# Output projection by seven products of quarters; quarter sums and a mask on GpSimd, layer 0's statistics on ScalarE

## The chip, the cores and the metric

The kernel runs on one core of one Trainium2 chip. The metric is the device time of one execution in microseconds. Each core has a matmul engine (TensorE, PE in the profile, with its weight loads listed as PEld), VectorE (DVE), ScalarE (ACT), GpSimd (POOL) and the queue of SyncE (SP), which issues transfers. Each works through its own instructions in order, and they wait for one another by semaphores.

## The reference

```python
def reference(x, adj, W, a_src, a_dst, Wq, bq, Wk, bk, Wv, bv, Wo, bo):   # x: (64, 256, 512) f32
    # layer 0: graph attention over 256 nodes, one head
    h = relu(layernorm(x))
    Wh = h @ W
    logits = leaky_relu((Wh @ a_src)[:, :, None] + (Wh @ a_dst)[:, None, :], 0.2)
    x = x + softmax(where(adj == 0, -inf, logits)) @ Wh
    # layer 1: 8 heads of 64, masked by adj
    h = relu(layernorm(x))
    q, k, v = heads(h @ Wq.T + bq), heads(h @ Wk.T + bk), heads(h @ Wv.T + bv)
    attn = softmax(where(adj == 0, -inf, q @ k.T / 8))
    return x + concat(attn @ v) @ Wo.T + bo
```

All arithmetic is in f32. The layer norm has no weights (eps 1e-5).

## The kernel before

One batch element g (256 tokens, two tiles of 128, four chunks of 128 features) is the unit of work; there are G = 64. Each stage is a Python generator (`normalize0`, `weights0`, `aggregate0`, `transform0`, `normalize1`, `transpose1`, `project_qk`, `project_v`, `attention`, `scale`, `output`) that issues the instructions of one step and yields. The lists `period`, `second`, `first` and `last` write out by hand in what order the steps of five batches in flight are issued; TensorE, VectorE, ScalarE and the SP queue keep that program order (`tc.manual_schedule(engines=...)`). A period is one pass through the lists. The letters: K is one of seven steps of `project_qk` for batch i, V one of seven of `project_v`, W one of four halves of layer 0's transform for i+1, O a step of `output` for i-2, N0, E0, U0 layer 0's statistics and normalization, edge weights and aggregation for i+2, N1, X1 layer 1's normalization and transposes for i+1, A and A_OLD the attention of i and of i-1.

q, k and v are made by a scheme of seven products (`products`): the left matrix and the weight are each cut into 2 x 2 quarters, `combine_w` makes sums of the weight's quarters once, `combine` makes four sums of the left's quarters per batch (128x256 each, all in SBUF), and `add_up` puts the seven results together on VectorE, which reads them from PSUM. Of `project_qk`'s products, number 0 and number 4 are read by ScalarE first, with a bias. For number 4, ScalarE writes the tile p5 (line 576), and VectorE then makes two additions from it (lines 203 and 204). The output projection is not done so before: `output` computes it with plain products, four halves (steps O) per batch, and adds each 128x512 result to the residual x (line 704), then stores it.

`normalize0` uses VectorE's batch-norm statistics (lines 99, 100), a power on GpSimd (line 106), ScalarE's normalizing ReLU (line 418) and four multiply-and-sum instructions on VectorE (line 425), which give the node scores es and ed. `weights0` begins with two TensorE transposes of es (line 439, the tile pe), then takes exponents on ScalarE, the maximum, the mask (line 453) and the sum of two halves (line 455) on VectorE. `attention` multiplies the exponents with the mask (line 627) and sums two halves (line 629) on VectorE; line 687 (`scale`) applies the reciprocals to aT. GpSimd also adds the output bias to x (line 551), in `transpose1`.

All PSUM tiles come from one pool of eight banks. The parts of the schedule that matter here:

```python
second = [
    W, N1, E0, K, W, W, N1, A_OLD, A, N1, E0, A, V, A, V, V, V, V, U0, V, V,
    X1, U0, X1, U0, X1, U0, A, A, (scale, -1),
]
period = [(load, 3), A_OLD, K, A_OLD, O, K, O, N0, K, O, N0, K, O, N0, K, W, K] + second
```

Of the kernel before, what the change touches and what calls it, by code (L numbers as in the profile page):

```python
# [9 lines left out]
F32 = mybir.dt.float32  # L10
# [6 lines left out]
P = 128  # L17
# [11 lines left out]
def kernel(  # L29
# [71 lines left out]

    def inverse_std(mv, nm, small):
        ve = small.tile([P, NT], F32, tag="ve", name=f"ve{nm}")
        nc.vector.tensor_scalar_add(ve, mv[:, :, 1], EPS)  # L104
        rstd = small.tile([P, NT], F32, tag="rstd", name=f"rstd{nm}")
        nc.gpsimd.tensor_tensor(rstd, ve, minus_half, op=ALU.pow)  # L106
        return rstd

    def norm_stats(xt, nm, small):

        mv = small.tile([P, NT, 2], F32, tag="mv", name=f"mv{nm}")
        for t in range(NT):
            token_stats(mv[:, t, :], xt[:, t, :], f"{nm}_{t}", small)
        return mv, inverse_std(mv, nm, small)

# [16 lines left out]
    def bounded():  # L132
# [10 lines left out]

        def load_w(src, name):
            t = weights.tile([P, DC, D], F32, tag=name, name=name)
            nc.sync.dma_start(t, src.rearrange("(c p) e -> p c e", p=P))
            return t

        def load_quarters(src, name):
# [17 lines left out]
        def combine(a, name):  # L167

            s = work.tile([P, 4, DC // 2, P], F32, tag=name[0], name="_".join(name))
            nc.vector.tensor_add(s[:, 0], a(1, 0), a(1, 1))  # L170
            nc.vector.tensor_sub(s[:, 1], s[:, 0], a(0, 0))  # L171
            nc.vector.tensor_sub(s[:, 2], a(0, 0), a(1, 0))
            nc.vector.tensor_sub(s[:, 3], a(0, 1), s[:, 1])
            return s
# [60 lines left out]
        load_group(0)  # L235
        w_sb = load_w(w, "w_sb")
        a_rows = [work.tile([P, D], F32, tag=f"aT{j}", name=f"a_row_{j}", bufs=2 - j) for j in range(2)]
# [7 lines left out]
        load_group(2)  # L245
        wo_sb = load_w(woT, "wo_sb")
        wv_sb = load_quarters(wvT, "wv_sb")
# [42 lines left out]
        def prepare_qk():  # L290
# [4 lines left out]
            combine_w(wk_sb)  # L295

        def output_bias():

            pb = bank([P, D], "pbias")
            for c in range(DC):  # L300
                nc.tensor.matmul(
                    pb,
                    cols["bv"][:, c : c + 1].to_broadcast([P, P]),
                    wo_sb[:, c, :],
                    start=(c == 0),
                    stop=(c == DC - 1),
                )
            nc.vector.tensor_add(bo_b, pb, bo_b)

        def constants():  # L310


            def whole(wt, src, nm):
                b12 = work.tile([P, DC // 2, HD], F32, tag="b12", name=f"b12_{nm}", bufs=2)
                nc.gpsimd.dma_start(b12, quarter_of(src, 0, 1))
                return ((wt[:, B11], b12), (wt[:, B21], wt[:, B22]))

# [79 lines left out]
            nc.vector.tensor_reduce(okm, ok, AX.X, ALU.min)  # L397
            yield
            pk = bank([1, 1], "pok")
# [5 lines left out]
        def normalize0(g):  # L405

            xt = xts[g]
            mv, rstd = norm_stats(xt, f"0_{g}", small)
            nmr = small.tile([P, NT], F32, tag="nmr", name=f"nmr_{g}")
            yield  # L410
            nc.vector.scalar_tensor_tensor(  # L411
                nmr, mv[:, :, 0], -1.0, rstd, op0=ALU.mult, op1=ALU.mult
            )
            h = big.tile([P, NT, D], F32, tag="h", name=f"h_{g}", bufs=2)
            es = small.tile([P, NT], F32, tag="es", name=f"es_{g}")
            ed = small.tile([P, NT], F32, tag="ed", name=f"ed_{g}")
            for t in range(NT):
                nc.scalar.activation(  # L418
                    h[:, t, :], xt[:, t, :], AF.Relu, bias=nmr[:, t : t + 1], scale=rstd[:, t : t + 1]
                )  # L420
            yield
            for t in range(NT):
                for dst, a in ((es, 0), (ed, 1)):
                    junk = work.tile([P, D], F32, tag="junk", name=f"junk_{g}_{t}")
                    nc.vector.scalar_tensor_tensor(
                        junk, h[:, t, :], 1.0, wa[a], op0=ALU.mult, op1=ALU.mult,
                        accum_out=dst[:, t : t + 1],
                    )
            edl = small.tile([P, NT], F32, tag="edl", name=f"edl_{g}")
            nc.vector.tensor_scalar_mul(edl, ed, NEG_SLOPE)  # L430
            nodes[g] = h, es, ed, edl
            yield

        def weights0(g):
# [17 lines left out]
            em = work.tile([P, NC, N], F32, tag="em", name=f"em_{g}", bufs=2)  # L452
            nc.vector.tensor_mul(em, e1, maskT)  # L453
            esum = work.tile([P, N], F32, tag="esum", name=f"esum_{g}")
            nc.vector.tensor_add(esum, em[:, 0, :], em[:, 1, :])
            edges[g] = em, esum
            yield

        def aggregate0(g):
# [26 lines left out]
            nc.vector.reciprocal(rs, rs)  # L486

            sums0[g] = uT, rs
            yield

        def project_half(dst, left, w_t, t, n):
# [23 lines left out]
        def normalize1(g):  # L515
            xt = xts[g]
            mv = small.tile([P, NT, 2], F32, tag="mv", name=f"mv1_{g}")
            for t in range(NT):
                token_stats(mv[:, t, :], xt[:, t, :], f"1_{g}_{t}", small)
                if t == 0:  # L520
                    yield
            rstd = inverse_std(mv, f"1_{g}", small)
            yield
# [12 lines left out]
        def transpose1(g):  # L536
            xn = norms.pop(g)
            hT = big.tile([P, DC, TOK], F32, tag="hT", name=f"hT_{g}")

            def a(t, j):  # L540
                return hT[:, 2 * j : 2 * j + 2, t * P : (t + 1) * P]

            for t in range(NT):
                pt = bank([P, DC, P], f"pt_{g}_{t}")
                for c in range(DC):
                    nc.tensor.transpose(pt[:, c, :], xn[:, t, c * P : (c + 1) * P], ident)
                nc.scalar.activation(hT[:, :, t * P : (t + 1) * P], pt, AF.Relu)
                yield
            lefts[g] = a, combine(a, ("hs", str(g)))
            for t in range(NT):  # L550
                nc.gpsimd.tensor_tensor(xts[g][:, t, :], xts[g][:, t, :], bo_b, op=ALU.add)  # L551
            yield
# [48 lines left out]
        def attention(g):  # L601
# [47 lines left out]
            for j in range(2):  # L649
                pair = [scores(2 * j + i) for i in range(2)]  # L650
                yield
                for i in range(2):
                    sums.append(masks(2 * j + i, pair[i]))
                    yield
                values(j, pair)
                if j == 0:
                    yield
# [26 lines left out]
        def scale(g):  # L684
# [3 lines left out]

            outs[g] = aT
            yield  # L690

        def output(g):
            xt = xts.pop(g)
            aT = outs.pop(g)

            def left(c, t):
                return aT[c // 2][:, c % 2, t * P : (t + 1) * P]

            for t in range(NT):
                po = bank([P, D], f"po1_{g}_{t}")  # L700
                project_half(po, left, wo_sb, t, 0)
                yield
                project_half(po, left, wo_sb, t, 1)
                nc.vector.tensor_add(xt[:, t, :], po, xt[:, t, :])  # L704
                row = (g * NT + t) * P
                nc.sync.dma_start(out_rows[row : row + P, :], xt[:, t, :])
                yield

# [20 lines left out]
        def aside(n=1):  # L729
# [8 lines left out]
        second = [  # L738
            W, N1, E0, K, W, W, N1, A_OLD, A, N1, E0, A, V, A, V, V, V, V, U0, V, V,
            X1, U0, X1, U0, X1, U0, A, A, (scale, -1),  # L740
        ]
        period = [(load, 3), A_OLD, K, A_OLD, O, K, O, N0, K, O, N0, K, O, N0, K, W, K] + second
        last = [A_OLD, A_OLD, A_OLD, O, O, O, O, (scale, -1)]


        steps((normalize0, 0), (normalize0, 0))
        node_weights()
        edge_mask()
        steps((normalize0, 0), (weights0, 0))
        aside()  # L750
        steps((normalize0, 1), (weights0, 0), (aggregate0, 0), (aggregate0, 0))
        prepare_qk()
        steps((aggregate0, 0), (aggregate0, 0), (normalize0, 1), (transform0, 0), (transform0, 0))
        steps((normalize1, 0), (transform0, 0), (transform0, 0), (normalize1, 0))
        aside(2)
# [4 lines left out]
        first = [  # L760
            (load, 3), K, (normalize0, 1), K, (weights0, 1), K, N0, K, (weights0, 1), N0, K,
            (aggregate0, 1), (aggregate0, 1), N0, K, (aggregate0, 1), (aggregate0, 1), W,
        ]
        for i in range(G + 2):
            for n, (stage, ahead) in enumerate(last if i == G else period if i else first + second):
# [217 lines left out]
```

## Time and profile before

| | us |
|---|---|
| median of three runs | 3026.2 (3024.74 to 3027.28) |
| the profiled execution's own time | 3028.91 |
| its span, from first to last instruction | 3027.1 |
| PE busy | 2987.1 (99%) |
| PEld busy | 2184.2 (72%) |
| DVE busy | 2124.1 (70%) |
| ACT busy | 941.3 (31%) |
| POOL busy | 296.5 (10%) |

The granted TensorE clock is 0.998 of full speed over the span. Rows of groups read: line, engine, operation, tiles written and read, shapes, count, then busy time and mean duration of one in ns, then the idle time before them. Rows of the timeline read: start and length in us from the span's start, engine, line, operation, tiles, shape, how many instructions are merged in the row, and in brackets the idle time before them with what ended it. One period of the steady state is 46.18 us: GpSimd's additions of line 551 start at 964.36 us and again at 1010.54 us.

### The profile page before, as it was taken

The page shows a single profiled execution, that of the slowest core. Times are in us where ns is not written, and L with a number is a line of the kernel's source. Part 1 is how long each engine was busy: PE and PEld are TensorE (multiplying, and loading weights), DVE is VectorE, ACT ScalarE, POOL GpSimd, SP SyncE. Part 2 cuts the span into 40 slices and gives each one's busy share as a digit, 9 for nine tenths or more (in the row PEclk, how much of TensorE's full clock was granted, in tenths as well). Part 3 has the DMA queues.
Part 4 walks back from the last instruction along what each step waited for, and adds up shares of the span by engine and source line. Part 5 has one row for each costly group of instructions (what it writes and reads, how often), then busy time and mean ns, then how long its engine had stood idle before and what let it go on. Part 6 is the DMA issues. An engine that isn't in the chain of part 4 may idle for free. (4 is left out here: it accounts for less than half of the span.)

```text
span 3027.1 us, 45790 instructions
## 1 busy us (share of the span) xinstructions
PE 2987.1 (99%) x18166; PEld 2184.2 (72%) x18166; DVE 2124.1 (70%) x4110; ACT 941.3 (31%) x2011; POOL 296.5 (10%) x279
## 2 busy tenths in 40 slices
PE   7999999999999999999999999999999999999998
PEld 5777777777777777777777777777777777777775
DVE  6767767767777677677677677776776776777764
ACT  2333323323333333233233333332332333333321
POOL 1100101101101101011011011010110110110100
PEclk9999999999999999999999999999999999999999
DMA  3112212212212122122122122221221221222213
GB/s 125 18 30 41 36 28 39 39 29 39 31 36 36 31 40 36 29 39 39 28 39 33 35 36 32 39 36 29 42 36 29 39 38 30 38 32 38 29 23 42
DMA packets 82062, 110.79 MB, mean 37 GB/s; under 512 B 11762, under 2 KB 47602, under 8 KB 81842
## 3 DMA queue, kind: packets, MB, share of 16 engines
q1 hardware_dynamic: 81122, 105.95, 21.9%
q8 instruction: 145, 2.38, 0.3%
q0 software_dynamic: 720, 1.85, 0.2%
q14 instruction: 75, 0.61, 0.1%
HBM read 40.64 MB, written 33.55 MB: 25 GB/s over the span
## 5 line engine op out<-in xcount | busy, mean ns | idle before, releaser
L493 PE MATMUL po<-wo_sb,aT 128*128 128x512 f32 x1024 | 483.0, 595 | 4.7 <-DVE aT L687 4.7
L493 PE MATMUL po<-w_sb,uT 128*128 128x512 f32 x1024 | 470.9, 593 | 0.0
L627 DVE TENSOR_TENSOR ex<-ex,maskT 128x512 f32<-128x512 f32 x512 | 397.0, 816 | 7.1 <-ACT ex L622 1.4
L221 PEld LDWEIGHTS pqk<-hs,wq_sb 128*128 128x128 f32 x2048 | 263.5, 192 | 90.3 <-issue 89.4
L106 POOL TENSOR_TENSOR rstd<-ve,minus_half 128x2 f32<-128x2 f32 x128 | 89.5, 699 | 2379.4 <-DVE ve L104 2379.4
L622 ACT ACTIVATE ex<-psc 128x512 f32<-128x512 f32 x512 | 264.4, 602 | 126.3 <-PE psc L614 126.3
L493 PEld LDWEIGHTS po<-w_sb,uT 128*128 128x128 f32 x1024 | 180.1, 191 | 154.4 <-issue 154.4
L493 PEld LDWEIGHTS po<-wo_sb,aT 128*128 128x128 f32 x1024 | 176.0, 192 | 132.6 <-issue 129.8
L221 PE MATMUL pqk<-hs,wq_sb 128*128 128x128 f32 x2048 | 270.1, 275 | 0.7 <-DVE hs L171 0.7
L221 PE MATMUL pqk<-hs,wk_sb 128*128 128x128 f32 x2048 | 270.5, 275 | 0.0
L510 DVE SCALAR_TENSOR_TENSOR x<-po,rs,x 128x512 f32<-128x512 f32 x128 | 96.1, 751 | 238.5 <-PE po L493 238.5
L614 PE MATMUL psc<-qk 64*128 64x256 f32 x2048 | 255.7, 389 | 0.0
L212 PE MATMUL pv<-wv_sb,hs 128*128 128x256 f32 x1024 | 254.5, 381 | 0.0
L221 PEld LDWEIGHTS pqk<-hT,wq_sb 128*128 128x128 f32 x1536 | 196.2, 191 | 80.4 <-issue 59.3
L639 PE MATMUL pav<-ex,v 128*64 128x256 f32 x2048 | 250.9, 386 | 3.0 <-DVE ex L627 2.4
L221 PEld LDWEIGHTS pqk<-hs,wk_sb 128*128 128x128 f32 x2048 | 249.3, 192 | 0.0
L468 PE MATMUL pu<-em,h 128*128 128x256 f32 x1024 | 241.9, 379 | 1.7 <-DVE em L453 1.0
L418 ACT ACTIVATE h<-x,nmr,rstd 128x512 f32<-128x512 f32 x128 | 97.1, 805 | 469.2 <-DVE nmr L411 469.2
L629 DVE TENSOR_TENSOR sm<-ex 128x512 f32<-128x512 f32 x256 | 235.1, 918 | 8.8
L614 PEld LDWEIGHTS psc<-qk 64*128 64x128 f32 x2048 | 187.3, 186 | 68.4 <-issue 26.2
L551 POOL TENSOR_TENSOR x<-x,bo_b 128x512 f32<-128x512 f32 x128 | 198.0, 1568 | 257.3 <-ACT xn L530 250.8
L647 ACT COPY aT<-pav 128x512 f32<-128x512 f32 x128 | 75.1, 586 | 472.5 <-PE pav L639 459.8
(147 smaller groups left out, 3935.7 us busy)
## 6 DMA issues: line engine op xcount, KB each, us to landing
x<-in_x_dram SPq DMA_DIRECT2D x64, 512.0 KB, 5.4
rb<-rc SPq DMA_DIRECT2D x512, 64.0 KB, 4.7
out_dram<-x SPq DMA_DIRECT2D x128, 256.0 KB, 2.0
w_sb<-in_L_gnn_W_dram SPq DMA_DIRECT2D x1, 1024.0 KB, 8.3
wq_sb<-in_L_gnn_Wq_dram SPq DMA_DIRECT2D x4, 256.0 KB, 14.6
wk_sb<-in_L_gnn_Wk_dram SPq DMA_DIRECT2D x4, 256.0 KB, 10.9
wo_sb<-in_L_gnn_Wo_dram SPq DMA_DIRECT2D x1, 1024.0 KB
wv_sb<-in_L_gnn_Wv_dram SPq DMA_DIRECT2D x4, 256.0 KB, 8.6
```

Source lines behind the costliest of these rows:

```text
L212: nc.tensor.matmul(dst[:, 0:HD], left[:, c, :], wt[:, slot, c, :], start=c == 0, stop=c == 1)
L221: nc.tensor.matmul(dst[:, at : at + P], wt[:, slot, c, e * P : (e + 1) * P], left[:, c, :], start=c == 0, stop=c == 1,)
L418: nc.scalar.activation(h[:, t, :], xt[:, t, :], AF.Relu, bias=nmr[:, t : t + 1], scale=rstd[:, t : t + 1])
L468: nc.tensor.matmul(pu[:, d, :], h[:, m, (dp + d) * P : (dp + d + 1) * P], em[:, m, :], start=(m == 0), stop=(m == NC - 1),)
L493: nc.tensor.matmul(dst, left(c, t), w_t[:, c, :], start=(c == 0), stop=(c == DC - 1))
L510: nc.vector.scalar_tensor_tensor(xt[:, t, :], po, rs[:, t : t + 1], xt[:, t, :], op0=ALU.mult, op1=ALU.add)
L551: nc.gpsimd.tensor_tensor(xts[g][:, t, :], xts[g][:, t, :], bo_b, op=ALU.add)
L614: nc.tensor.matmul(psc[r][:, m, :], qk[rows, 2 + e % 2, m * P : (m + 1) * P], qk[rows, e % 2, :], start=True, stop=True,)
L622: nc.scalar.activation(ex[:, r, :, :], psc[r], AF.Exp, scale=SCALE)
L627: nc.vector.tensor_mul(ex[:, r, :, :], ex[:, r, :, :], maskT)
L629: nc.vector.tensor_add(sm, ex[:, :, 0, :], ex[:, :, 1, :])
L639: nc.tensor.matmul(pav[r * DH : (r + 1) * DH, i, :], v[j][:, m, at : at + DH], pair[i][:, r, m, :], start=(m == 0), stop=(m == NC - 1),)
```

## The change

- `output` becomes seven products through `products`, with `wo_sb` loaded by quarters and its sums made once by `combine_w` in the second pass. Each product is 128x256 and is added from PSUM straight into every quarter of x that it belongs to (one instruction of one to four quarters: 1024, 768, 256, 512, 512, 256 and 256 elements per partition). The sums of aT's quarters are made in `scale`.
- `combine` runs on GpSimd; so do the mask product and the half sum of `weights0`. GpSimd joins the engines that keep program order. The bias addition moves from `transpose1` into `attention`, ahead of its first mask product.
- `normalize0` has four steps: ScalarE copies with accumulated sums, VectorE scales them to means; ScalarE squares with accumulated sums, VectorE and GpSimd make the inverse deviation; the normalizing ReLU; the node scores.
- The order lists are rewritten; there are seven O and four N0 per period.

```diff
-    def inverse_std(mv, nm, small):
+    def inverse_std(var, nm, small, scale=1.0):
         ve = small.tile([P, NT], F32, tag="ve", name=f"ve{nm}")
-        nc.vector.tensor_scalar_add(ve, mv[:, :, 1], EPS)
+        nc.vector.tensor_scalar(ve, var, scale, EPS, op0=ALU.mult, op1=ALU.add)
...
         def combine(a, name):
             s = work.tile([P, 4, DC // 2, P], F32, tag=name[0], name="_".join(name))
-            nc.vector.tensor_add(s[:, 0], a(1, 0), a(1, 1))
-            nc.vector.tensor_sub(s[:, 1], s[:, 0], a(0, 0))
-            nc.vector.tensor_sub(s[:, 2], a(0, 0), a(1, 0))
-            nc.vector.tensor_sub(s[:, 3], a(0, 1), s[:, 1])
+            nc.gpsimd.tensor_tensor(s[:, 0], a(1, 0), a(1, 1), op=ALU.add)
+            nc.gpsimd.tensor_tensor(s[:, 1], s[:, 0], a(0, 0), op=ALU.subtract)
+            nc.gpsimd.tensor_tensor(s[:, 2], a(0, 0), a(1, 0), op=ALU.subtract)
+            nc.gpsimd.tensor_tensor(s[:, 3], a(0, 1), s[:, 1], op=ALU.subtract)
...
-        wo_sb = load_w(woT, "wo_sb")
+        wo_sb = load_quarters(woT, "wo_sb")
...
         def output_bias():
+            wo_q = whole(wo_sb, woT, "o")
             pb = bank([P, D], "pbias")
-            for c in range(DC):
-                nc.tensor.matmul(pb, ..., wo_sb[:, c, :], ...)
+            for j in range(2):
+                for c in range(DC):
+                    nc.tensor.matmul(pb[:, j * HD : (j + 1) * HD], ..., wo_q[c // 2][j][:, c % 2, :], ...)
...
         def normalize0(g):
             xt = xts[g]
-            mv, rstd = norm_stats(xt, f"0_{g}", small)
-            nmr = small.tile([P, NT], F32, tag="nmr", name=f"nmr_{g}")
-            yield
-            nc.vector.scalar_tensor_tensor(
-                nmr, mv[:, :, 0], -1.0, rstd, op0=ALU.mult, op1=ALU.mult
-            )
...
+            for t in range(NT):
+                nc.scalar.activation(
+                    h[:, t, :], xt[:, t, :], AF.Copy, accum_out=nmean[:, t : t + 1]
+                )
+            nc.vector.tensor_scalar_mul(nmean, nmean, -1.0 / D)
+            yield
+            for t in range(NT):
+                nc.scalar.activation(
+                    h[:, t, :], xt[:, t, :], AF.Square, bias=nmean[:, t : t + 1],
+                    accum_out=ssq[:, t : t + 1],
+                )
+            rstd = inverse_std(ssq, f"0_{g}", small, 1.0 / D)
+            yield
+            nmr = small.tile([P, NT], F32, tag="nmr", name=f"nmr_{g}")
+            nc.vector.tensor_mul(nmr, nmean, rstd)
             for t in range(NT):
                 nc.scalar.activation(h[:, t, :], xt[:, t, :], AF.Relu, ...)
...
         def weights0(g):
-            nc.vector.tensor_mul(em, e1, maskT)
+            nc.gpsimd.tensor_tensor(em, e1, maskT, op=ALU.mult)
-            nc.vector.tensor_add(esum, em[:, 0, :], em[:, 1, :])
+            nc.gpsimd.tensor_tensor(esum, em[:, 0, :], em[:, 1, :], op=ALU.add)
...
         def transpose1(g):
             lefts[g] = a, combine(a, ("hs", str(g)))
-            for t in range(NT):
-                nc.gpsimd.tensor_tensor(xts[g][:, t, :], xts[g][:, t, :], bo_b, op=ALU.add)
...
         def attention(g):
                 pair = [scores(2 * j + i) for i in range(2)]
                 yield
+                if j == 0:
+                    for t in range(NT):
+                        part = xts[g][:, t, :]
+                        nc.gpsimd.tensor_tensor(part, part, bo_b, op=ALU.add)
...
         def scale(g):
-            outs[g] = aT
+            outs[g] = a, combine(a, ("as", str(g)))
...
         def output(g):
-            for t in range(NT):
-                po = bank([P, D], f"po1_{g}_{t}")
-                project_half(po, left, wo_sb, t, 0)
-                yield
-                project_half(po, left, wo_sb, t, 1)
-                nc.vector.tensor_add(xt[:, t, :], po, xt[:, t, :])
...
+            quarters = xt.rearrange("p t (j d) -> p (t j) d", j=2)
+            where = (
+                quarters, quarters[:, 1:4, :], quarters[:, 0:1, :], quarters[:, 2:4, :],
+                quarters[:, 1:4:2, :], quarters[:, 2:3, :], quarters[:, 1:2, :],
+            )
...
+            def read(n, ps):
+                dst = where[n]
+                nc.vector.tensor_add(dst, spread(ps, [P, dst.shape[1], HD]), dst)
+                if n >= 5:
+                    store(6 - n)
+
+            yield from products(a, s, f"po1_{g}", partial(product_rows, wo_sb), read)
...
         second = [
-            W, N1, E0, K, W, W, N1, A_OLD, A, N1, E0, A, V, A, V, V, V, V, U0, V, V,
-            X1, U0, X1, U0, X1, U0, A, A, (scale, -1),
+            E0, K, O, A_OLD, A, E0, W, W, N1, V, W, W, N1, V, V, N1, A, V, A,
+            U0, V, V, U0, V, X1, X1, X1, U0, U0, A, A, (scale, -1),
         ]
-        period = [(load, 3), A_OLD, K, A_OLD, O, K, O, N0, K, O, N0, K, O, N0, K, W, K] + second
+        period = [
+            (load, 3), A_OLD, K, A_OLD, O, K, N0, O, K, N0, O, K, N0, O, K, O, N0, K, O,
+        ] + second
...
+                if i == 1 and n == 8:
+                    combine_w(wo_sb)
...
             mybir.EngineType.PE, mybir.EngineType.DVE, mybir.EngineType.Activation,
-            mybir.EngineType.SP,
+            mybir.EngineType.SP, mybir.EngineType.Pool,
```

More of the change, by code (lines that the diff above doesn't have):

```diff
@@ L113, in norm_stats @@
             token_stats(mv[:, t, :], xt[:, t, :], f"{nm}_{t}", small)
-        return mv, inverse_std(mv, nm, small)
+        return mv, inverse_std(mv[:, :, 1], nm, small)
     def project_rows(dst, hT, w_t, t):
@@ L142, in bounded @@
         B11, B21, B22, T1, T2, T3, T4N = range(7)
[L144 to L147, printed above, removed]
         def load_quarters(src, name):
@@ L235, in bounded @@
         load_group(0)
-        w_sb = load_w(w, "w_sb")
+        w_sb = weights.tile([P, DC, D], F32, tag="w_sb", name="w_sb")
+        nc.sync.dma_start(w_sb, w.rearrange("(c p) e -> p c e", p=P))
         a_rows = [work.tile([P, D], F32, tag=f"aT{j}", name=f"a_row_{j}", bufs=2 - j) for j in range(2)]
@@ L295, in prepare_qk, with whole @@
             combine_w(wk_sb)
+        def whole(wt, src, nm):
+            b12 = work.tile([P, DC // 2, HD], F32, tag="b12", name=f"b12_{nm}", bufs=2)
+            nc.gpsimd.dma_start(b12, quarter_of(src, 0, 1))
+            return ((wt[:, B11], b12), (wt[:, B21], wt[:, B22]))
         def output_bias():
+            wo_q = whole(wo_sb, woT, "o")
             pb = bank([P, D], "pbias")
-            for c in range(DC):
[L301 to L306, printed above, removed]
-                )
+            for j in range(2):
+                for c in range(DC):
+                    nc.tensor.matmul(
+                        pb[:, j * HD : (j + 1) * HD],
+                        cols["bv"][:, c : c + 1].to_broadcast([P, P]),
+                        wo_q[c // 2][j][:, c % 2, :],
+                        start=(c == 0),
+                        stop=(c == DC - 1),
+                    )
             nc.vector.tensor_add(bo_b, pb, bo_b)
         def constants():
[L313 to L316, printed above, removed]
             ok = weights.tile([P, 2 * DC + 5], F32, tag="ok", name="ok")
@@ L397, in constants @@
             nc.vector.tensor_reduce(okm, ok, AX.X, ALU.min)
-            yield
+            for _ in range(12):
+                yield
             pk = bank([1, 1], "pok")
@@ L407, in normalize0 @@
             xt = xts[g]
-            mv, rstd = norm_stats(xt, f"0_{g}", small)
-            nmr = small.tile([P, NT], F32, tag="nmr", name=f"nmr_{g}")
-            yield
-            nc.vector.scalar_tensor_tensor(
-                nmr, mv[:, :, 0], -1.0, rstd, op0=ALU.mult, op1=ALU.mult
-            )
             h = big.tile([P, NT, D], F32, tag="h", name=f"h_{g}", bufs=2)
@@ L416, in normalize0 @@
             ed = small.tile([P, NT], F32, tag="ed", name=f"ed_{g}")
+            nmean = small.tile([P, NT], F32, tag="nmean", name=f"nmean_{g}")
+            ssq = small.tile([P, NT], F32, tag="ssq", name=f"ssq_{g}")
+            for t in range(NT):
[10 more added lines that the diff above has]
+            rstd = inverse_std(ssq, f"0_{g}", small, 1.0 / D)
+            yield
+            nmr = small.tile([P, NT], F32, tag="nmr", name=f"nmr_{g}")
+            nc.vector.tensor_mul(nmr, nmean, rstd)
             for t in range(NT):
@@ L489, in aggregate0, with spread @@
             yield
+        def spread(ps, shape):
+            return ps[:, 0:HD].unsqueeze(1).to_broadcast(shape)
         def project_half(dst, left, w_t, t, n):
@@ L521, in normalize1 @@
                     yield
-            rstd = inverse_std(mv, f"1_{g}", small)
+            rstd = inverse_std(mv[:, :, 1], f"1_{g}", small)
             yield
@@ L687, in scale, with a @@
                 nc.vector.tensor_mul(aT[j], aT[j], rb[:, 2 * j : 2 * j + 2, :])
-            outs[g] = aT
+            def a(t, j):
+                return aT[j][:, :, t * P : (t + 1) * P]
+            outs[g] = a, combine(a, ("as", str(g)))
             yield
@@ L693, in output, with store @@
             xt = xts.pop(g)
-            aT = outs.pop(g)
-            def left(c, t):
-                return aT[c // 2][:, c % 2, t * P : (t + 1) * P]
-            for t in range(NT):
-                po = bank([P, D], f"po1_{g}_{t}")
-                project_half(po, left, wo_sb, t, 0)
-                yield
-                project_half(po, left, wo_sb, t, 1)
-                nc.vector.tensor_add(xt[:, t, :], po, xt[:, t, :])
+            a, s = outs.pop(g)
+            quarters = xt.rearrange("p t (j d) -> p (t j) d", j=2)
+            where = (
+                quarters, quarters[:, 1:4, :], quarters[:, 0:1, :], quarters[:, 2:4, :],
+                quarters[:, 1:4:2, :], quarters[:, 2:3, :], quarters[:, 1:2, :],
+            )
+            def store(t):
                 row = (g * NT + t) * P
                 nc.sync.dma_start(out_rows[row : row + P, :], xt[:, t, :])
-                yield
+            def read(n, ps):
[4 more added lines that the diff above has]
+            yield from products(a, s, f"po1_{g}", partial(product_rows, wo_sb), read)
         def load(g):
@@ L738, in bounded @@
         second = [
-            W, N1, E0, K, W, W, N1, A_OLD, A, N1, E0, A, V, A, V, V, V, V, U0, V, V,
-            X1, U0, X1, U0, X1, U0, A, A, (scale, -1),
-        ]
-        period = [(load, 3), A_OLD, K, A_OLD, O, K, O, N0, K, O, N0, K, O, N0, K, W, K] + second
-        last = [A_OLD, A_OLD, A_OLD, O, O, O, O, (scale, -1)]
-        steps((normalize0, 0), (normalize0, 0))
+            E0, K, O, A_OLD, A, E0, W, W, N1, V, W, W, N1, V, V, N1, A, V, A,
+            U0, V, V, U0, V, X1, X1, X1, U0, U0, A, A, (scale, -1),
+        ]
+        period = [
+            (load, 3), A_OLD, K, A_OLD, O, K, N0, O, K, N0, O, K, N0, O, K, O, N0, K, O,
+        ] + second
+        last = [A_OLD, A_OLD, A_OLD, O, O, O, O, O, O, O, (scale, -1)]
+        steps((normalize0, 0), (normalize0, 0), (normalize0, 0))
         node_weights()
@@ L750, in bounded @@
         aside()
-        steps((normalize0, 1), (weights0, 0), (aggregate0, 0), (aggregate0, 0))
+        steps((normalize0, 1), (weights0, 0), (normalize0, 1), (aggregate0, 0), (aggregate0, 0))
+        steps((aggregate0, 0), (aggregate0, 0), (normalize0, 1))
         prepare_qk()
-        steps((aggregate0, 0), (aggregate0, 0), (normalize0, 1), (transform0, 0), (transform0, 0))
-        steps((normalize1, 0), (transform0, 0), (transform0, 0), (normalize1, 0))
+        steps((transform0, 0), (transform0, 0), (transform0, 0), (transform0, 0))
+        steps((normalize1, 0), (normalize1, 0))
         aside(2)
@@ L760, in bounded @@
         first = [
-            (load, 3), K, (normalize0, 1), K, (weights0, 1), K, N0, K, (weights0, 1), N0, K,
-            (aggregate0, 1), (aggregate0, 1), N0, K, (aggregate0, 1), (aggregate0, 1), W,
+            (load, 3), K, (normalize0, 1), K, (weights0, 1), K, N0, K, (weights0, 1), N0, K, N0,
+            (aggregate0, 1), (aggregate0, 1), N0, K, (aggregate0, 1), (aggregate0, 1),
         ]
```

## The prediction

> **What bounds the kernel now.** The page's first part comes first:
>
> ```profile
> PE 2987.1 (99%) x18166; PEld 2184.2 (72%) x18166; DVE 2124.1 (70%) x4110; ACT 941.3 (31%) x2011; POOL 296.5 (10%) x279
> ```
>
> TensorE works for 99% of the span. The list of waits confirms that the others wait for it: of VectorE's waits, the ones on matmuls are longest (line 510 on po 238.5 us, line 704 on po 130.8 us), while TensorE's own are some 27 us in all, at the start and the end. So time falls only with TensorE's work, and rises with every new wait of TensorE, in full. TensorE's timeline of one steady period gives the length of each slot:
>
> ```profile
> 980.61 1.05 PE L221 MATMUL pqk<-hs,wq_sb 128*128 128x128 f32 x8
> 982.39 1.88 PE L493 MATMUL po<-wo_sb,aT 128*128 128x512 f32 x4
> 984.11 1.05 PE L221 MATMUL pqk<-hT,wq_sb 128*128 128x128 f32 x8
> ...
> 1014.61 1.03 PE L212 MATMUL pv<-wv_sb,hT 128*128 128x256 f32 x4
> 1015.47 1.03 PE L212 MATMUL pv<-wv_sb,hs 128*128 128x256 f32 x4
> 1016.34 0.60 PE L546 MATMUL pt<-ident,xn 128*128 128x128 f32 x4
> ```
>
> From start to start, a K slot is 1.78 us (980.61 to 982.39), an old O slot 1.72 (to 984.11), a V product 0.865 (1014.61 to 1016.34 for two). Rows overlap, so starts are compared, not lengths.
>
> Two more views are needed. The timeline of all engines shows, early in the run, VectorE waiting for ScalarE's p5 and going on to the node scores at once (start, length, columns as before):
>
> ```profile
> 60.83 1.12 ACT L576 ACTIVATE p<-pqk,bias 128x128 f32<-128x128 f32 x4
> 61.98 0.69 DVE L203 TENSOR_TENSOR qk<-qk,p 128x512 f32<-128x512 f32 x1 [2.61 <-ACT p L576]
> 62.58 0.69 DVE L204 TENSOR_TENSOR qk<-s,p 128x512 f32<-128x512 f32 x1
> 63.19 0.68 DVE L425 SCALAR_TENSOR_TENSOR junk<-h,wa 128x512 f32<-128x512 f32 x1
> 63.91 0.69 DVE L425 SCALAR_TENSOR_TENSOR junk<-h,wa 128x512 f32<-128x512 f32 x1
> 64.65 0.69 DVE L425 SCALAR_TENSOR_TENSOR junk<-h,wa 128x512 f32<-128x512 f32 x1
> 65.27 0.08 DVE L425 DVE_READ_ACCUMULATOR junk<-h,wa 128x1 f32 x1
> ```
>
> The same timeline shows TensorE waiting there for the third score of the four, which completes es:
>
> ```profile
> 52.13 0.08 DVE L425 DVE_READ_ACCUMULATOR junk<-h,wa 128x1 f32 x1
> 52.24 0.69 DVE L425 SCALAR_TENSOR_TENSOR junk<-h,wa 128x512 f32<-128x512 f32 x1
> 52.26 0.32 PE L439 MATMUL pe<-ident,es 128*128 128x128 f32 x1 [0.59 <-DVE junk L425]
> ```
>
> VectorE's timeline shows its masks beside GpSimd's two additions of line 551, which run from 1010.54 to 1013.64, and without them:
>
> ```profile
> 1010.15 2.36 DVE L627 TENSOR_TENSOR ex<-ex,maskT 128x512 f32<-128x512 f32 x2
> 1012.55 1.64 DVE L629 TENSOR_TENSOR sm<-ex 128x512 f32<-128x512 f32 x1
> 1014.11 1.28 DVE L627 TENSOR_TENSOR ex<-ex,maskT 128x512 f32<-128x512 f32 x2
> 1015.42 0.69 DVE L629 TENSOR_TENSOR sm<-ex 128x512 f32<-128x512 f32 x1
> ```
>
> One pair of heads takes 3.96 us (1010.15 to 1014.11) instead of 1.92 (1014.11 to 1016.03): two GpSimd additions cost VectorE 2.0 us where its operands both lie in SBUF.
>
> **The change part by part.** Per batch, on TensorE: four old O slots, 4 x 1.72 = 6.88 us, become seven of 0.865 = 6.06. Saved: 0.82 us, x64 = 52.5 us. This is all that the change can bring, since nothing else removes TensorE work.
>
> VectorE loses `combine` (109.4 us in its four rows / 64 = 1.71 us per batch), mask and half sum (44.2 + 29.1, 1.15 us), half of the batch-norm rows ((175.0 + 46.7) / 2, 1.73 us) and line 704 (88.5, 1.38 us): 5.97 us. It gains the seven reads. Rows from PSUM give 0.688 us for 512 elements and 0.415 for 256, so 1.07 ns per element: 1024 is 1.23, 768 is 0.96, two of 512 are 1.38, three of 256 are 1.25, together 4.82 us, and one small instruction of 0.17. Net 1.0 us less of 33.2 per batch. VectorE isn't the bound, so this is worth nothing by itself. What counts is what TensorE waits for.
>
> **The new wait.** In the old order, K, W, K, W and N1 stood around and after the scores; the third score's accumulator was read by 994.15 and pe ran at 998.12: 3.97 us to spare. The new order is K (product 4), O, N0 (scores), K, O, E0 (pe). From the end of product 4's matmuls, TensorE has O 0.865 + K 1.78 + O 0.865 = 3.51 us of work until pe. VectorE, in program order, must do ahead of es: wait for p5, lines 203 and 204, the read of O's product 4, then three scores. By the rows:
> - ScalarE starts p5 0.26 us after the matmuls (992.90 to 993.16 in the steady state), takes 1.14, and VectorE starts 0.03 later: 1.43.
> - Lines 203 and 204: 61.98 to 63.19, 1.21: 2.64.
> - The read of O's fourth product, 512 elements from PSUM: 0.60 (line 704 at 991.32, next at 991.92): 3.24.
> - Three scores with accumulators: 63.19 to 65.35, 2.16: 5.40. TensorE starts 0.05 later: 5.45.
>
> 5.45 - 3.51 = 1.94 us in which TensorE stands, once per period. Queued behind pe are K's last product, O's last, the attention values and all that follows; nothing fills the gap.
>
> **Is p5 itself late?** ScalarE's normalizing ReLU stands ahead of it. I count from the first score matmul of the period's last A step; product 4 then ends at 1.93 (scores) + 5 x 1.78 + 4 x 0.865 = 14.30, and p5 may start at 14.56. VectorE starts A_OLD's masks at 1.8 (1021.25 to 1023.05 now), or 2.1 if the new hs sums stretch the product with rb; two pairs take 3.84, plus 2.0 because the aT sums on GpSimd (as many elements as line 551's) now lie beside them: 7.9. Then the reads of O's first product 1.2 and of K's second 0.6, the mean 0.2; the squares on ScalarE 1.9 (two at 0.76 as in line 418, two accumulator reads at 0.2); the variance 0.3, GpSimd's power 0.7 with 0.1 to 0.4 of waiting, 0.2 for line 411's successor, and the ReLU 0.1 + 1.52. Sum: 7.9 + 2.0 + 1.9 + 1.3 + 0.2 + 1.6 = 14.9. This is 0.3 us late at most of my values; uncertain by 1 us to either side, and early costs nothing. I take 0.2. The wait is then 2.1 us.
>
> [...] The row before has one table load in the run, of 1.283 us. [...]
>
> **The other edits.** x + bo_b beside the first masks: it lay beside them before too (1010.54), price 0, and TensorE's values have then to wait for V's fifth read. From the last W slot: rows up to the masks 3.1, two pairs 1.9 x 2 + 2.0, three V reads 1.6: 10.5 us, against 9.95 us of TensorE slots before the values and 0.47 of values that need only the first token tile: 0.1 us, up to 0.8. The mask and half sum on GpSimd (twice line 551's 1.27 to 1.73 us at most) have over 8 us of W and V slots until U0; hs's sums (four of 0.65 to 0.9 us) have scores and values, 3.8 us, and K's first product; the aT sums the first K and O; each covered, at 0.1 to 0.5 us per batch if not. Copies on ScalarE lie beside masks. The last batches need the aT sums in the open, about 2 us, against shorter products: 0. In the opening, statistics on ScalarE cost 1.3 us more than on VectorE, and four sums of `wo_sb` 2.7 us of VectorE once: +3 at most, taken with the end as 0. SP's queue has its stores ahead of rb's transfers, which have more time until `scale` than before.
>
> **Sum**, against the profiled execution's 3028.9 us: - 52.5 + 62 x 2.1 (130; pe of the first two batches lies in the opening) + 62 x 0.1 (6) = 3112.6. The median lies 2.7 lower: 3110 us. With the wait between 1.5 and 2.7, this case spans 3073 to 3147.
>
> **Rivals.**
> - Faster: no wait decides, and TensorE's saving comes through. It needs the wait at pe below 0.82 us, so es 1.1 us sooner than the rows allow, as when VectorE's order lets the scores pass p5. For it: 70% busy VectorE, relieved by 1.0 us; 3.97 us to spare before. Against: line 203 is ahead in program order, and the early rows show exactly this queue. Price: 3026 - 52 = 2974.
> - Slower still: GpSimd's eight sums per batch beside masks, or a table load (1.283 us each), put p5 1 to 2.6 us late, or V's reads come late by 0.8: 3150 to 3250. Decided by whether the ReLU ends after 14.56.
> - The products don't get cheaper: if each costs 0.97 us as the first V slot after scores does (1008.46 to 1009.43), seven are 6.79, the saving 0.09, and with the wait the time is 3157.
> - The two cancel (wait near 0.8): 3026.
>
> **How the numbers follow.** Forecast 0.70, faster 0.11, slower still 0.13, dear products 0.04, cancelled 0.02. About 0.2% (6 us) is what a measurement tells here. Slower by more: 0.87; faster 0.11; within 0.02. The range, 3062 to 3185, holds the forecast and half of the slower case. If a part of the wait is missing I'd expect it near the low end.
>
> **What would show it.** Right: a wait of pe (line 439) on the scores some 1.9 us long in nearly every period, 110 to 140 us in all, PE's busy share near 94%; O products 0.865 from start to start; p5 ending just before lines 203 and 204; masks at 2.4 us a pair beside GpSimd's sums. Wrong: TensorE without gaps at E0; the scores done before K's fifth product; O slots over 0.9 us; a second ACT_TABLE_LOAD.

## The result, and the profile after

The changed kernel takes 3097.45 us (median of four, 3097.1 to 3097.98) against 3025.86 us for the kernel before: a ratio of 1.0236, 95% interval 1.0219 to 1.0254. It is slower, by 71.6 us; 84 us was forecast. The profiled execution took 3097.98 us, with a span of 3096.2.

The first part of its page (busy time of each engine, share of the span, instructions):

```profile
PE 2963.7 (96%) x18942; PEld 2325.9 (75%) x18942; DVE 2228.2 (72%) x3858; ACT 1130.9 (37%) x2523; POOL 932.2 (30%) x920
```

TensorE is busy for less time than before (2963.7 us against 2987.1) in a longer span: it stands. TensorE's timeline of one steady period shows where (start, length, then the idle time before the row with what ended it):

```profile
1004.10 1.03 PE L207 MATMUL po<-wo_sb,as 128*128 128x256 f32 x4
...
1006.75 1.03 PE L207 MATMUL po<-wo_sb,aT 128*128 128x256 f32 x4
1008.13 0.29 PE L450 MATMUL pe<-ident,es 128*128 128x128 f32 x1 [0.35 <-DVE junk L436]
1009.50 0.32 PE L450 MATMUL pe<-ident,es 128*128 128x128 f32 x1 [1.08 <-DVE junk L436]
1009.66 1.06 PE L216 MATMUL pqk<-hs,wq_sb 128*128 128x128 f32 x8
```

K's product 4 ends at 1004.10, where the next O starts. O's product 5 would end by slots at 1006.75 + 0.865 = 1007.61, pe takes 0.22 undisturbed (998.12 to 998.34 before), so K's last product could start at 1007.83; it starts at 1009.66, 1.83 us later. The two transposes wait for the first and third of the four scores. The timeline of all engines shows what VectorE does meanwhile:

```profile
1002.51 1.52 ACT L429 ACTIVATE h<-x,nmr,rstd 128x512 f32<-128x512 f32 x2 [1.44 <-DVE nmr L427]
...
1004.30 1.14 ACT L589 ACTIVATE p<-pqk,bias 128x128 f32<-128x128 f32 x4 [0.28 <-PE pqk L216]
...
1005.48 0.69 DVE L198 TENSOR_TENSOR qk<-qk,p 128x512 f32<-128x512 f32 x1 [2.27 <-ACT p L589]
...
1006.69 0.68 DVE L727 TENSOR_TENSOR x<-po,x 128x512 f32<-128x512 f32 x1
...
1007.29 0.68 DVE L436 SCALAR_TENSOR_TENSOR junk<-h,wa 128x512 f32<-128x512 f32 x1
...
1009.37 0.08 DVE L436 DVE_READ_ACCUMULATOR junk<-h,wa 128x1 f32 x1
```

This is the predicted queue, item by item: VectorE idles 2.27 us for p5, then makes its two additions (line 198 and the next), reads O's product 4, and only then the scores, although the ReLU that gives h had ended at 1004.03. The steady period, from one reciprocal of `scale` to the next (line 687; line 670 before), is 47.27 us against 46.18 before: +1.09 us, and the 59 periods of this length make 64.2 of the 69.1 us by which the span grew. The opening and the end, with four periods of other lengths, make the other 4.9.

### The profile page after: what moved, and what is told of

It reads as the page before. It is cut to its first block, busy times and chain, and to the rows that moved or that the text cites. A ratio compares the mean times of both kernels' runs of the same rounds, so it can differ in the third digit from the quotient of the medians.

```text
span 3096.2 us, 48277 instructions
## 1 busy us (share of the span) xinstructions
PE 2963.7 (96%) x18942; PEld 2325.9 (75%) x18942; DVE 2228.2 (72%) x3858; ACT 1130.9 (37%) x2523; POOL 932.2 (30%) x920
## 4 chain that ended last, share of the span: by engine, by line
PE 87%; DVE 8%; ACT 2%; issue 2%; DMA 1%; SPq 0%; POOL 0%; DVEq 0%; POOLq 0%; ACTq 0%
PE pqk L216 23%; PE po L508 15%; PE pv L207 12%; PE po L207 9%; PE psc L627 8%; PE pav L652 8%; PE pu L479 7%; DVE junk L436 4%; ACT p L589 2%; PE psm L679 2%; PE pt L561 2%; DVE qk L199 1%; DVE x L727 1%; PE ps L492 1%; PE pe L450 1%
## 5 line engine op out<-in xcount | busy, mean ns | idle before, releaser
L640 DVE TENSOR_TENSOR ex<-ex,maskT 128x512 f32<-128x512 f32 x512 | 515.3, 1046 | 56.8 <-ACT ex L635 56.6
L464 POOL TENSOR_TENSOR em<-e,maskT 128x512 f32<-128x512 f32 x64 | 81.3, 1270 | 981.2 <-DVE e L462 975.7
L508 PEld LDWEIGHTS po<-w_sb,uT 128*128 128x128 f32 x1024 | 189.3, 190 | 208.3 <-issue 184.5
L727 DVE TENSOR_TENSOR x<-po,x 128x256 f32<-128x256 f32 (+3 forms) x448 | 307.1, 686 | 22.9 <-PE po L207 16.2
L207 PE MATMUL po<-wo_sb,as 128*128 128x256 f32 x1024 | 264.1, 381 | 4.4 <-POOL as L166 4.4
L652 PE MATMUL pav<-ex,v 128*64 128x256 f32 x2048 | 258.0, 390 | 8.9 <-DVE v L201 6.3
L207 PE MATMUL pv<-wv_sb,hs 128*128 128x256 f32 x1024 | 262.5, 379 | 0.0
L545 ACT ACTIVATE xn<-x,nmr,rstd 128x512 f32<-128x512 f32 x128 | 97.2, 807 | 451.8 <-DVE nmr L540 451.8
L207 PEld LDWEIGHTS pv<-wv_sb,hs 128*128 128x128 f32 x1024 | 194.6, 190 | 53.3 <-issue 30.1
L687 DVE RECIPROCAL rc<-psm 128x256 f32<-128x256 f32 x64 | 112.5, 1757 | 155.5 <-PE psm L679 155.5
```

Of the source, the lines that this page charges most:

```text
L207: nc.tensor.matmul(dst[:, 0:HD], left[:, c, :], wt[:, slot, c, :], start=c == 0, stop=c == 1)
L508: nc.tensor.matmul(dst, left(c, t), w_t[:, c, :], start=(c == 0), stop=(c == DC - 1))
L545: nc.scalar.activation(norms[g][:, t, :], xt[:, t, :], AF.Identity, bias=nmr[:, t : t + 1], scale=rstd[:, t : t + 1],)
L640: nc.vector.tensor_mul(ex[:, r, :, :], ex[:, r, :, :], maskT)
L652: nc.tensor.matmul(pav[r * DH : (r + 1) * DH, i, :], v[j][:, m, at : at + DH], pair[i][:, r, m, :], start=(m == 0), stop=(m == NC - 1),)
L687: nc.vector.reciprocal(rc, psm)
```

## Experiments

Wait theory: TensorE's wait at pe costs 1.83 us per period, the seven products save 0.82, nothing else counts. Rivals: GpSimd's new work slows VectorE's masks (the row of the mask products grew from 397.0 to 515.3 us, more than the whole loss); the relief of VectorE, not the products, is where a gain would come from.

**pe one K and one O later.**

```diff
-            E0, K, O, A_OLD, A, E0, W, W, ...
+            K, O, E0, A_OLD, A, E0, W, W, ...
```

> The changed kernel with the step E0 (transposes of the node scores, pe) issued one K and one O later. Wait theory: TensorE has 2.65 us more to do before pe, more than the 1.83 us that it stands there now, so the wait goes and nothing else moves: 3097.5 - 62 x 1.83 = 2984 us. Contention theory (GpSimd's sums slow VectorE's masks, whose row grew from 397 to 515 us, and TensorE pays for that): masks and GpSimd's work are the same, so about 3097 us, less at most a few us.

Measured: 2988.93 us, ratio to before 0.9884 (0.9867 to 0.9900). The period is 45.43 us, 1.83 less than the changed kernel's. That is 5 us above the 2984 expected: the 59 steady periods gain 108 of the 113 us counted for 62, and the first period gains 0.54 only (45.13 to 44.59), since TensorE waits 2.54 us for a read of V there instead. TensorE's timeline:

```profile
1022.61 1.03 PE L207 MATMUL po<-wo_sb,as 128*128 128x256 f32 x4
1023.48 0.38 PE L450 MATMUL pe<-ident,es 128*128 128x128 f32 x2
1023.79 1.95 PE L652 MATMUL pav<-ex,v 128*64 128x256 f32 x16
```

Both transposes run in one piece, with no idle time before them. Moving one list entry by two places turns a loss into a gain of 35 us, with all the GpSimd and ScalarE work in place. The wait is shown, and GpSimd's contention with the masks isn't what made the change slow.

**The scores ahead of product 4.**

```diff
-            ..., N0, O, K, O, N0, K, O,
+            ..., N0, O, N0, K, O, K, O,
```

> The changed kernel with the last step of N0 (the four score instructions) issued before K's product 4 instead of after it and the O that follows, all else in place. Wait theory, and in it the claim that the scores are late because p5's wait, two additions and a read of O stand ahead of them: the ReLU ends 0.3 us before p5 may start, so es is complete about 2.1 us after product 4's matmuls end instead of 5.4, against 3.5 us of matmuls: no wait, 2984 us. If the scores were late for another reason (late ReLU), part of the 1.83 us stays. Contention theory: about 3097 us.

Measured: 2988.64 us, 0.9882 (0.9866 to 0.9899). VectorE's timeline shows the fourth score's accumulator and the p5 addition in the other order:

```profile
1018.63 0.08 DVE L436 DVE_READ_ACCUMULATOR junk<-h,wa 128x1 f32 x1
1018.75 0.17 DVE L441 TENSOR_SCALAR edl<-ed 128x2 f32<-128x2 f32 x1
1018.83 0.68 DVE L198 TENSOR_TENSOR qk<-qk,p 128x512 f32<-128x512 f32 x1
```

pe follows at 1020.00 without a gap, and the period is 45.44 us. The scores were late only because VectorE keeps program order and stood for p5; h had been ready.

**One O after pe instead of before it.**

```diff
-            ..., O, N0, K, O,   ] + [ E0, K, O, A_OLD, ...
+            ..., O, N0, K,      ] + [ E0, O, K, O, A_OLD, ...
```

> The changed kernel with one O product issued after pe instead of before it. Wait theory: TensorE has 0.865 us less to do while VectorE works, VectorE's queue ahead of es is the same, so the wait is 2.7 us: 3097.5 + 62 x 0.865 = 3151 us. Contention theory: about 3097 us.

Measured: 3166.45 us, 1.0472 (1.0454 to 1.0489): 69 us over the changed kernel, not 54. Most periods are 48.13 us, 0.86 more, as expected; 11 of them are 49.75. TensorE's timeline of one of these:

```profile
1075.23 0.29 PE L450 MATMUL pe<-ident,es 128*128 128x128 f32 x1 [1.21 <-DVE junk L436]
1076.61 0.32 PE L450 MATMUL pe<-ident,es 128*128 128x128 f32 x1 [1.08 <-DVE junk L436]
1076.77 1.03 PE L207 MATMUL po<-wo_sb,aT 128*128 128x256 f32 x4
1077.64 1.68 PE L216 MATMUL pqk<-hs,wq_sb 128*128 128x128 f32 x8
1079.11 1.91 PE L216 MATMUL pqk<-hs,wk_sb 128*128 128x128 f32 x8
```

and busy time by stretch, with the granted clock as third number from the end:

```profile
1074.00:1078.00 4.00, 1.71 (x10) 1.42 (x10) 3.86 (x12) 0.95 (x3) 0.00 (x0) 0.99 0.00 0
1078.00:1081.40 3.40, 3.40 (x17) 3.31 (x16) 0.75 (x3) 0.73 (x2) 0.00 (x0) 0.51 0.20 77
```

After the wait the clock was granted at half rate for 3.4 us, and the K product took 3.17 us (1077.64 to 1080.81) instead of 1.78. So 59 x 0.86 + 11 x 1.63 = 69 us, as measured. The mechanism was right; a second cost came with the longer wait.

**pe a further K and O earlier**, to see whether that second cost grows.

```diff
-            ..., O, K, O, N0, K, O,   ] + [ E0, K, O, A_OLD, ...
+            ..., O, K, O, N0, E0, K, O,   ] + [ K, O, A_OLD, ...
```

> The changed kernel with E0 (pe) issued directly after the scores, one K and one O earlier, which makes the wait longer by 1.78 + 0.865 = 2.65 us, 4.48 us per period. By the wait alone: 3097.5 + 61 x 2.65 = 3259 us. In e3_o_after_pe, with 2.69 us of wait, 12 of 60 periods were 1.63 us longer still, each beside 3.4 us in which the granted clock is 0.5; at 1.83 us none were. If that grows with the idle time, more periods carry 1.6 us: 12 to 61 of them, 3279 to 3360 us. If it was chance: 3259 us.

(The twelfth stretch that this text counts lies at the end of the run, outside the steady periods, of which there are 59.) Measured: 3339.85 us, 1.1039 (1.1022 to 1.1056), 81 us over what the wait alone gives, and in the range for a cost that grows. Most periods are 51.20 us: 47.27 + 2.65 + 1.28. TensorE's timeline:

```profile
1027.33 1.03 PE L207 MATMUL po<-wo_sb,as 128*128 128x256 f32 x4
1031.35 0.29 PE L450 MATMUL pe<-ident,es 128*128 128x128 f32 x1 [2.99 <-DVE junk L436]
1032.73 0.47 PE L450 MATMUL pe<-ident,es 128*128 128x128 f32 x1 [1.09 <-DVE junk L436]
1032.99 1.92 PE L216 MATMUL pqk<-hT,wq_sb 128*128 128x128 f32 x8
1034.70 1.42 PE L216 MATMUL pqk<-hT,wk_sb 128*128 128x128 f32 x8
```

Each of the 59 steady periods now has a stretch of half clock at the end of the wait and behind it (the mean granted clock is 0.965 against 0.997), and the K product shown takes 2.97 us (1032.99 to 1035.96). With one exception the stretches of neighbouring periods start 51.20 us apart, and all but two last 3.41 us (those two 6.83); 51.20 is 15.0 times 3.41. So the period is a multiple of the stretch's length here, and the 1.28 us looks, as an estimate from this run alone, like the rest up to the next multiple (47.27 + 2.65 = 49.92 is 14.6 times 3.41) and not like a fixed price; no other length was tried.

**Quarter sums on VectorE again**, else the changed kernel.

```diff
-            nc.gpsimd.tensor_tensor(s[:, 0], a(1, 0), a(1, 1), op=ALU.add)
+            nc.vector.tensor_add(s[:, 0], a(1, 0), a(1, 1))        # and the other three
```

> The changed kernel with the quarter sums (combine, hs and as) on VectorE again. Wait theory: VectorE has 3.4 us more per batch, the masks are faster by some 2 us, neither lies between product 4 and pe: 3097 us, within 8. Contention theory: the masks' row falls back toward 400 us and the time with it, to 3030 to 3060 us.

Measured: 3097.3 us, 1.0241 (1.0224 to 1.0258), the same. The masks' group of this kernel (busy us, mean ns of one, idle before):

```profile
L640 DVE TENSOR_TENSOR ex<-ex,maskT 128x512 f32<-128x512 f32 x512 | 397.7, 817 | 2.2 <-ACT ex L635 2.2
```

The same group in the changed kernel:

```profile
L640 DVE TENSOR_TENSOR ex<-ex,maskT 128x512 f32<-128x512 f32 x512 | 515.3, 1046 | 56.8 <-ACT ex L635 56.6
```

So the contention is real, 118 us of VectorE's time, and costs nothing: the masks don't lie between product 4 and pe. The rival falls.

**Bias addition earlier**, on top of the later pe: x + bo_b as a step of its own after E0's second step.

```diff
-            K, O, E0, A_OLD, A, E0, W, W, ...            # x + bo_b inside A, ahead of the masks
+            K, O, E0, A_OLD, A, E0, (bias, 0), W, W, ...
```

> e1_pe_later with the bias addition (x + bo_b on GpSimd) issued after E0's second step, when VectorE has no work with two operands in SBUF, instead of ahead of the first masks. Contention as a second, small wait: in e1 the attention values stand 0.09 us per period for V's fifth read, because two GpSimd additions stretch the masks by 1.1 us and the small line 540 from 0.1 to 1.2 us; with them gone, VectorE is 2 us earlier there and the 0.09 x 61 = 5 us go: 2983.5 us. If the wait has another cause: 2989 us.

Measured: 2973.48 us, 0.9832 (0.9818 to 0.9845), the fastest here, 51 us under the kernel before. The period falls from 45.43 to 45.35 us, 5 us in all, as expected; the other 10 us are one period at each end of the run (44.59 to 40.29 and 48.82 to 43.08), which I had not expected. The two traces show what went: in these periods TensorE's waits for a read of V fall from 2.54 to 0.17 us and from 4.62 to 1.52, and the stretches of half clock beside the longer waits (3.41 us from 137.3, 6.83 from 2908.9) are gone. That the V reads stand open there because fewer other steps cover them is likely and wasn't tried. Line 540, an instruction on two elements per partition, in the kernel with the later pe alone:

```profile
L540 DVE SCALAR_TENSOR_TENSOR nmr<-mv,rstd 128x2 f32<-128x2 f32 x64 | 76.3, 1192 | 0.0
```

and with the addition moved:

```profile
L540 DVE SCALAR_TENSOR_TENSOR nmr<-mv,rstd 128x2 f32<-128x2 f32 x64 | 10.3, 161 | 0.0
```

**Statistics on VectorE again**, with the later pe (batch-norm instructions in N0's first step, the second step empty).

```diff
-            for t in range(NT): nc.scalar.activation(h[:, t, :], xt[:, t, :], AF.Copy, accum_out=...)
-            ...                                     # means, squares, inverse deviation
+            mv, rstd = norm_stats(xt, f"0_{g}", small)
```

> e1_pe_later with layer 0's statistics on VectorE's batch-norm instructions again (same four steps of N0, the second one empty). Theory that only TensorE's work and its waits count: VectorE has 1.6 us more per batch in a stretch with slack, ScalarE 3.2 us less: 2989 us, within 4. Rival, that the relief of VectorE carries part of the gain: 2995 to 3030 us.

Measured: 2994.0 us, 0.9900 (0.9885 to 0.9915), between the two forecasts (2985 to 2993, and 2995 to 3030); its interval overlaps that of the kernel with the later pe. The period is 45.52 instead of 45.43, with a new small wait of weight loads of the scores on VectorE's reads:

```profile
PEld psc L617 <- DVE x L717: 24.3, 59, 0.4
```

If anything, the move to ScalarE is worth 5 us, not the gain.

**The old output projection**, with the later pe and all else of the change.

```diff
-            yield from products(a, s, f"po1_{g}", partial(product_rows, wo_sb), read)
+            for t in range(NT): ...                 # two halves of plain products, one addition, as before the change
```

> e1_pe_later with the output projection as before the change (four halves of plain products, in the places of O's steps 2, 4, 5 and 6), all other parts kept. Theory: the seven products save 6.88 - 6.06 = 0.82 us of TensorE per batch and are the only source of gain: 2989 + 61 x 0.82 = 3039 us, a few us less for the shorter end. Rival, that the moved work or the order brings the gain: 2989 to 3015 us.

Measured: 3030.97 us, 1.0021 (1.0012 to 1.0030). The period is 46.265 us against 45.434: the seven products save 0.83 us per batch, and without them moved work and new order together are slightly slower than the kernel before. The forecast was 8 us too high: 59 periods are of the steady length, not 61, and the rest of the span is 299 us here and 306 with the seven products, more than the few us allowed for.

**All moves undone**, with the later pe: sums, mask product, half sum and statistics on VectorE.

```diff
-            nc.gpsimd.tensor_tensor(em, e1, maskT, op=ALU.mult)
+            nc.vector.tensor_mul(em, e1, maskT)     # and esum; combine and normalize0 as in the two edits above
```

> e1_pe_later with all moves undone: quarter sums, mask product, half sum and statistics on VectorE, so that only the seven products and the order are left (the bias addition stays where the change has it). Theory: VectorE has some 6 us more per batch, 39 of 45.4 us, and still no chain that TensorE waits for grows by more than its slack: 2989 us, within 8. Rival, that the seven reads of O need the relief: over 3000 us, with waits of TensorE on VectorE.

Measured: 2992.4 us, 0.9896 (0.9881 to 0.9911). VectorE is busy 80% of the span (2379.1 us) and TensorE 99%. The products and the order alone bring nearly the whole gain; the moves bring 3.5 us, within the intervals.

**The last batch's sums on VectorE**, on top of the earlier bias.

```diff
+            combine(a, ("as", str(g)), nc.vector if g == G - 1 else None)
```

> e5_bias_early with the aT sums of the very last batch on VectorE instead of GpSimd. In e5 TensorE waits 4.3 us in all for the last batch's sums on GpSimd, in the open; in e4, with the sums on VectorE, 2.9 us. Theory: 1.5 to 3 us less, 2971 us, nothing in the periods. If the last batch's wait is set by the transfers of rb: 2973.5 us.

Measured: 2975.5 us, 0.9835 (0.9822 to 0.9849): no difference that can be told, so the 1.5 to 3 us did not come. TensorE's wait there is 3.4 us instead of 4.3, and the span is the same 2973.0.

## Why the prediction was right

Direction, mechanism and place were right; the forecast of 3110 was 12.6 us above the measured median, inside the range. By its steps:

- **The saving.** 0.82 us per batch from slots; 0.83 by the two kernels that differ in the output projection and the places of its steps (46.265 - 45.434). O slots are 0.865 us from start to start, so the rival of dear products falls.
- **The wait at pe.** The chain from product 4's end to pe was put at 5.45 us; it is 5.40 (1004.10 to 1009.50), and the 3.51 us of slots are as counted. Taking the wait away moves the period by 1.83 us. The idle time alone is less than forecast, 0.35 + 1.08 = 1.43 us per period and 89.1 us in all for 110 to 140, and PE is busy 96% of the span for 94%: the first transpose and the end of O's row lie inside the wait and count as busy. The 1.94 was 0.1 too much: pe's first transpose runs during the wait, so only the second is left (0.16 us to K's next start instead of 0.22), and the chain is 0.05 shorter.
- **p5 late by 0.2: wrong, the mis-sized term.** p5 started at 1004.30 because the matmuls had ended, 0.27 us after the ReLU was done. My count put the ReLU at 14.9 us from the A step's scores; it ended at 14.34 (1036.95 to 1051.29, the first ReLU row of the next period at 1049.77 plus 1.52). Masks and mean were as counted (masks over at 8.0, forecast 7.9), by luck in part: the masks started at 1.80 instead of 2.1, and GpSimd's sums cost them 2.4 us instead of 2.0. The two squares with their accumulator reads took 1.53 us (1046.83 to 1048.36), not 1.9: the reads of 0.19 lie partly beside the squares. The power came after 0.1 of waiting, the low end. p5 started at 14.62, not 14.56: K's first product takes 1.89 us from start to start (1038.88 to 1040.77) instead of 1.78, and ScalarE follows the matmuls by 0.20 instead of 0.26. With 1.83 for 2.1, the sum would have been 3096 us instead of 3113, against the profiled execution's 3098. ScalarE's timeline of the changed kernel:

```profile
1046.83 0.72 ACT L420 ACTIVATE h<-x,nmean 128x512 f32<-128x512 f32 x1 [3.49 <-DVE nmean L417]
1047.45 0.19 ACT L420 ACTIVATION_READ_ACCUMULATOR h<-x,nmean 128x1 f32 x1
1047.55 0.71 ACT L420 ACTIVATE h<-x,nmean 128x512 f32<-128x512 f32 x1
1048.16 0.19 ACT L420 ACTIVATION_READ_ACCUMULATOR h<-x,nmean 128x1 f32 x1
1049.77 1.52 ACT L429 ACTIVATE h<-x,nmr,rstd 128x512 f32<-128x512 f32 x2 [1.43 <-DVE nmr L427]
1051.57 1.14 ACT L589 ACTIVATE p<-pqk,bias 128x128 f32<-128x128 f32 x4 [0.28 <-PE pqk L216]
```

- **V's fifth read, 0.1 us per period**: 0.08 measured, by moving its cause; in the changed kernel the attention values take 1.96 us from start to start (1034.99 to 1036.95), against 1.88 before (1019.37 to 1021.25). The opening and the end, put at 0, cost 4.9 us of span.
- **TensorE's own waits before**, read as some 27 us, are 34 us in the list. They lie outside the steady periods, as said, and nothing rests on the sum.
- **Rivals.** The faster case was priced at 2974: 2988.9 was reached when the wait alone was taken away, 2973.5 when the bias moved too. The slower case's trigger, the ReLU after 14.56, missed by 0.2 us. GpSimd's eight sums did slow VectorE, and did not reach TensorE; GpSimd's bias addition did, by the 0.08 us.

The slower rival's 2.6 us is the length of two table loads of 1.283 us, and no run shows a load that comes with Square: Exp, Copy, Relu and Square run in the changed kernel with a single ACT_TABLE_LOAD of 1.283 us in the whole run (line 414), and the kernel before, without Square, has one of the same length (line 418).

## What to carry to other kernels

Where one engine is 99% busy, count for every step that is moved what the other engines have queued ahead of its input, in program order, and compare it with that engine's own work in between: both sums can be made from start-to-start times of the trace before, and here came within 0.1 us of what was measured. The longer count over three engines, up to the ReLU, was off by 0.6 us. A wait that isn't the step's own (p5 ahead of the scores) counted in full (1.83 us per period, 47.27 to 45.44, with the scores ahead of it), and moving an entry of a hand-written order by two places can be worth more than the change it belongs to. Relieving an engine that isn't waited for brought 0 to 5 us, however many busy microseconds moved; the 15 us of the earlier bias addition came where TensorE did wait for VectorE.

## What the runs showed of the hardware that was not expected

- **Behind waits of 2.7 us and more, TensorE's clock was granted at half rate for a time.** With 1.83 us of wait per period, no steady period had half clock. With 2.69 us, 11 of 59 had, every fifth or sixth; from one to the next it was 242.3 or 290.1 us. With 4.48 us all 59 had. In the steady periods each stretch lasted 3.4 us, or twice that, and the periods grew by 1.3 to 1.6 us.
- As an estimate, 242.3 and 290.1 us are 71 and 85 times the 3.41 us of a stretch, each to within 0.1, as the 51.20 us above are 15.0 times; why just these 11 periods were hit is not shown by a run of its own. In the period shown for the O after pe, TensorE had 2.9 us ahead of the half clock with two short transposes in them and no other matmul (1073.86, where the last K slot ends, to 1076.77).
- **A tiny VectorE instruction took as long as the GpSimd instruction beside it.** Line 540, two operands in SBUF and two elements per partition, took 1.19 us on average beside GpSimd's additions and 0.16 with them moved away. In the changed kernel's timeline it runs from 1027.97 to 1029.19, and the addition beside it takes 1.27 us from 1027.90.
- GpSimd's 128x256 half sum (line 466) took 0.72 us with VectorE idle (at 1019.15, where VectorE idles until 1020.95), and its 128x256 quarter sums 1.05 to 1.18 beside VectorE's masks (1039.13 to 1043.71 in the changed kernel's timeline); over the run a mask takes 1046 ns on average with them against 817 with the sums on VectorE: both sides lose.
